# A graph layer on one core: ScalarE issues the stores of the projected rows, and four pieces of an order written by hand move

## The chip, the cores and the metric

The kernel runs on one core of a Trainium2 chip: TensorE (PE), VectorE (DVE), ScalarE (ACT), GpSimd (POOL) and SyncE (SP), each with its own queue that it works through in order, and 16 DMA engines. The metric is the device time of one execution in microseconds. Before the change the median of three runs is 816.37 us (815.54 to 817.31).

## The reference

12,500 nodes with 128 features, 400,000 edges sorted by their destination. Each edge has a length; the weights of an edge come from a two-layer network over 50 radial functions of the length, times a cutoff that is zero beyond a length of 10.

```python
rbf = jnp.exp(-(distances[:, None] - centers) ** 2 / (2.0 * width * width))
cut = 0.5 * (jnp.cos(jnp.pi * distances / CUTOFF) + 1.0) * (distances <= CUTOFF)
W = (jax.nn.silu(rbf @ fw1 + fb1) @ fw2 + fb2) * cut[:, None]
messages = (h[src] @ pw + pb) * W
agg = jax.ops.segment_sum(messages, dst, num_segments=num_atoms)
h1 = h + (jax.nn.silu(agg @ mw1 + mb1) @ mw2 + mb2)
out = layernorm(x + h1)
```

## The kernel before

Only edges with a length up to 10 count. The kernel packs them: seven chunks of rows of edges (`pack(c)`) are compacted on VectorE in log steps (L410 to L439), scattered by POOL to a DRAM tile `packed` (L462), loaded again as `pair` (L479) and turned into four things by place: the indices of the sources `srci` (L533), the destinations within a window `dl` (L556), the window's base `base_i` (L560), and the cutoffs `cut` (L568 to L582). The lengths go back to DRAM as `near_d` (L490), from where they are broadcast to `d` (L656). Chunk 0 uses POOL for the last two transfers, the others SP. `pack` is a generator: each `yield` hands back an estimated time, and a planner advances it piece by piece between other work. `awake[c]` is the planner's time before which chunk c isn't advanced, `clock[0]` its time on VectorE, `pool[0]` that on POOL. The planner decides the order in which each engine gets its instructions; at run time the engines follow that order and wait on semaphores.

The packed edges are worked in quads of 512 (141 of them) and octs of two quads. Quads 0 to 6 belong to chunk 0, 7 to 25 to chunk 1, 26 to 47 to chunk 2 (the third).

The first stage multiplies all node rows by `pw` (`project`, 25 tiles of four times 128 nodes): the x tile is loaded by SP, transposed on TensorE (L595), copied by ScalarE (L597), multiplied (L274, L277), copied to `hp` by ScalarE (L608) and stored to the DRAM tensor `proj` by SP (`node_dma`, L137). `load_x` runs four tiles ahead, `turn` two tiles. The first eight quads are gathered from x itself, so that they need not wait for `proj`; their rows are transposed and multiplied in `multiply`, for four of them between the tiles. In the same loop the planner advances chunks 0 and 1 and the start of chunk 2, and the last four tiles also carry `ahead`: the radial functions of octs 0 and 1 (`basis`: two ScalarE operations over `d`, the second with Exp), their first layer (`first`, L693, on TensorE) and `silu` (L699, ScalarE).

The main loop goes over the quads. For quad q it issues gathers of later quads (L643, four on POOL for each quad, from `proj`, up to eight ahead until quad 24 and four from there; a gather may start when the buffer's last message is done), the second layer of quad q+2 (`second`, L707 and L710), the message (L717), one-hot matrices of the destinations (`place`, L726), the sums by TensorE (`sum_up`, L742) and their addition into `aggT` (L765). At `q % 4 == 3` it calls `basis` for octs q//4\*2+4 and q//4\*2+5; `basis` first drives the planner on (`go_on`) until the chunks of these quads have stored their lengths. The last gathered quads are followed by the node layers and the normalisation, of which most have been spread over the second half of the main loop.

Of the kernel before, what the change touches and what calls it, by code (L numbers as in the profile page):

```python
# [57 lines left out]
def kernel(  # L58
# [37 lines left out]
    nc = tc.nc  # L96
# [21 lines left out]
    def load_x(t0, name="x4", bufs=8):  # L118
        t = work.tile([P, 4, H], F32, name=name, bufs=bufs)
        node_dma(t0, t, x, False)  # L120
        x_sb[t0] = t

    def rows(t0, n=4):
        return [min(P, N - t * P) for t in range(t0, min(t0 + n, NT))]

    def alike(r):


        full = sum(1 for m in r if m == P)
        return [v for v in ((0, full, P), (full, len(r) - full, r[-1])) if v[1]]  # L130

    def node_dma(t0, sb, dr, store):

        for a, m, k in alike(rows(t0)):
            d = dr[(t0 + a) * P:(t0 + a) * P + m * k].rearrange("(t p) f -> p t f", p=k)
            s = sb[:k, a:a + m]
            nc.sync.dma_start(d, s) if store else nc.sync.dma_start(s, d)  # L137

    raw = {}

# [21 lines left out]
    def clear_packed(k, eng):  # L162
        a, b = CLEAR[k:k + 2]
        for i in range(3):
            v = packed[i, a:b].rearrange("(p w) -> p w", p=P)
            for w0 in range(0, (b - a) // P, 376):
                n = min(376, (b - a) // P - w0)
                eng.dma_start(v[:, w0:w0 + n], zero_i[:, :n])
# [6 lines left out]
    def clear(pieces=1, to=N):  # L175

        while pieces and to_clear and to_clear[0][0] < to:
            a, b = to_clear.pop(0)
            nc.scalar.activation(aggT[:, a:b], iota_n[:, :b - a], AF.Copy, scale=0.0)
            pieces -= 1  # L180
# [80 lines left out]
    def part_of(name, t, k, less=True):  # L261

        p = keep.tile([96, H], BF16, name=f"{name}_p{k}")
        nc.scalar.copy(p, t)
        nc.scalar.copy(bias_b[name][32 * k:32 * k + 1],
                       p[32 * k:32 * k + 1, None, :].to_broadcast([1, 4, H]))
        if k < 2 and less:
            nc.vector.tensor_sub(t, t, p)
        return lambda: nc.vector.tensor_sub(t, t, p)

    def rows_times(to, lT, w, bias_b, r):

        for a, c, m in alike(r):
            nc.tensor.matmul(to[:m, a:a + c, :], ones_b[:, :m], bias_b[:, :c, :], start=True,  # L274
                             stop=False)
            for k in range(a, a + c):
                nc.tensor.matmul(to[:m, k, :], lT[:, k * P:k * P + m], w, start=False,  # L277
                                 stop=(k == a + c - 1))
# [22 lines left out]
    proj = dram.tile([N, H], F32, name="proj")  # L301
# [5 lines left out]
    def bank():  # L307

        while not free:
            go_on(held[0])  # L310
        return free.pop(0)
# [29 lines left out]
    clock = [4.2]  # L341
# [3 lines left out]
    awake = [0.0] * NC_  # L345
# [14 lines left out]
    def pack(c):  # L360
# [12 lines left out]
        first = work.tile([P, 1], F32, name="first")  # L373
# [36 lines left out]
        for b in range(bits):  # L410
# [8 lines left out]
            k = 1 << b  # L419
# [126 lines left out]
        if c < WIDE_C:  # L546
# [30 lines left out]
        yield 0.42  # L577
        nc.vector.scalar_tensor_tensor(inside, f_dl, float(W), inside, op0=OP.is_lt, op1=OP.mult,
                                       accum_out=took[:np_, c:c + 1])
        yield 0.42  # L580
        nc.vector.scalar_tensor_tensor(f_cut, f_cut, -1.0, mark, op0=OP.add, op1=OP.mult)
        yield from to_places(f_cut, cut)  # L582
# [18 lines left out]
    def project(t0):  # L601
        r = rows(t0)
        b = bank()
        h = b.rearrange("p (k f) -> p k f", k=4)
        rows_times(h, xT_of.pop(t0), pw_sb, bias_b["pb"], r)
        hp = work.tile([P, 4, H], F32, name="hp", bufs=3)
        for a, c, m in alike(r):
            nc.scalar.copy(hp[:m, a:a + c], h[:m, a:a + c])  # L608
        free.append(b)
        node_dma(t0, hp, proj, True)  # L610

    def multiply(q):

# [34 lines left out]
    def quads(o):  # L648

        return [q for q in (2 * o, 2 * o + 1) if q < NQ]  # L650

    def radial(o, lengths, eng=None):

        d = work.tile([P, QE], F32, name="d", bufs=3)
        for h, ap in enumerate(lengths):
            (eng or nc.sync).dma_start(d[h * 64:h * 64 + 64], ap.to_broadcast([64, QE]))  # L656
        d_of[o] = d, len(lengths)
# [3 lines left out]
    def radials(to):  # L661

        while next_o[0] < min(to, -(-NQ // 2)):
            o = next_o[0]
            if not all(chunk_of(q) in stored for q in quads(o)):
                break
            radial(o, [near_d[2 * q:2 * q + 2].rearrange("(o p) e -> o (p e)", o=1)
                       for q in quads(o)])
            next_o[0] += 1

    def chunk_of(q):
        return max(c for c in range(NC_) if QB[c] <= q)

    def basis(o):
        if o not in d_of:
            for q in quads(o):
                while chunk_of(q) not in stored:
                    go_on(todo[0])
            radials(o + 1)
        d, n = d_of.pop(o)  # L680
        u = n * 64
        rbf = work.tile([P, QE], F32, name="rbf")
        nc.scalar.activation(rbf[:u], d[:u], AF.Square, bias=rbf_bias[:u], scale=rbf_scale[:u])  # L683
        nc.scalar.activation(rbf[:u], rbf[:u], AF.Exp, scale=-1.0 / (2.0 * width * width))  # L684
        rbf_of[o] = rbf, n

    def first(o):

        rbf, n = rbf_of.pop(o)
        ph = ps.tile([P, 2, QE], F32, name="ph", bufs=1)  # L690
        for h in range(n):
            p0 = h * 64
            nc.tensor.matmul(ph[:, h, :], w1_sb[p0:p0 + KR], rbf[p0:p0 + KR], start=True, stop=True)  # L693
        ph_of[o] = ph, n

    def silu(o):
        ph, n = ph_of.pop(o)
        s = work.tile([P, 2, QE], F32, name="s", bufs=3)
        nc.scalar.activation(s[:, :n], ph[:, :n], AF.Silu)  # L699
        for h in range(n):  # L700
            s_of[2 * o + h] = s[:, h]

    def second(q):

        s = s_of.pop(q)
        pu = bank()
        nc.tensor.matmul(pu, ones_b[:, :P], bias_b["fb2"].rearrange("k j f -> k (j f)"), start=True,  # L707
                         stop=False)
        for j in range(QT):
            nc.tensor.matmul(pu[:, j * H:(j + 1) * H], s[:, j * P:(j + 1) * P], fw2_sb,  # L710
                             start=False, stop=(j == QT - 1))
        pu_of[q] = pu
# [236 lines left out]
    tiles = list(range(0, NT, 4))  # L949
    def go_on(c):  # L950
        v = next(chunks[c], None)
        if v is None:
            todo.remove(c)
        else:
            clock[0] += v

    def pack_until(us, among=2):

        while clock[0] < us and todo and todo[0] < among:
            have = [c for c in todo[:2] if c < among]  # L960
            c = next((c for c in have if awake[c] <= clock[0]), None)
            if c is None:
                clock[0] = min([us] + [awake[c] for c in have])
            else:
                go_on(c)
# [18 lines left out]
    tensor = 8.0  # L984

    def ahead(k):

        if k < 2:
            basis(k)
        if k > 1:  # L990
            first(k - 2)
            silu(k - 2)

    for k, t0 in enumerate(tiles):
        if k + AHEAD_X < len(tiles):
            load_x(tiles[k + AHEAD_X])
        if loads and k >= 4 and k % 2 == 0:
            nc.sync.dma_start(*loads.pop(0))
        if k == 12:
            clear_packed(1, nc.sync)  # L1000
        if k in (16, 19, 22):
            if k > 16:
                take_off()
                clock[0] += 0.3
            take_off = part_of("fb2", fb2_f, (k - 16) // 3, False)
        if k == 17:
            load_rows(2)
            awake[2] = tensor + 10.0
        project(t0)
        clear(1, CLEARED)  # L1010
        if k + 2 < len(tiles):
            turn(tiles[k + 2])
        tensor += 2.25
        among = 2 if k < 17 else 3
        pack_until(tensor, among)
        fetches(tensor, FROM_X)
        while times[0] < min(fetched[0], 4) and there_at[times[0]] <= tensor:
            multiply(times[0])
            times[0] += 1
            tensor += 2.1  # L1020
            pack_until(tensor, among)
            fetches(tensor, FROM_X)
        if k in (17, 20, 23):
            radials((k - 14) // 3)
        if k >= len(tiles) - 4:
            ahead(k - len(tiles) + 4)
    while known[0] < QB[2]:
        go_on(todo[0])
    assert not loads
    fetches(clock[0], FROM_X)  # L1030
    for q in (0, 1):
        second(q)
    basis(2)
    basis(3)
    place(0)
# [144 lines left out]
```

## Time and profile before

| | |
|---|---|
| median of three runs | 816.37 us |
| the profiled execution's own time | 819.14 us |
| its span, from first to last instruction | 817.3 us |
| mean granted TensorE clock | 0.851 |
| POOL busy | 569.8 us (70%) |
| TensorE matmul busy | 604.2 us (74%) |
| VectorE busy | 587.5 us (72%) |
| ScalarE busy | 381.1 us (47%) |

No engine is busy all the time. The busy time by stage (microseconds of each engine in each stretch, from the profile's table by windows) shows how the stages differ:

| stretch | PE | DVE | ACT | POOL | PE clock | DMA share |
|---|---|---|---|---|---|---|
| 0 to 41 | 28.6 | 34.0 | 23.5 | 11.6 | 1.00 | 0.80 |
| 41 to 61 | 15.5 | 13.1 | 7.6 | 15.5 | 0.78 | 0.68 |
| 61 to 86 | 17.9 | 7.8 | 18.1 | 12.3 | 0.77 | 0.83 |
| 91 to 135 | 37.3 | 32.4 | 25.1 | 33.5 | 0.96 | 0.44 |
| 135 to 160 | 18.3 | 24.4 | 13.9 | 18.9 | 1.00 | 0.27 |
| 160 to 215 | 42.5 | 49.5 | 23.9 | 42.8 | 0.84 | 0.39 |
| 215 to 785 | 426.5 | 411.0 | 260.5 | 434.7 | 0.85 | 0.38 |

POOL counts as busy only while an instruction runs; between two gathers there is a gap of 0.30 us, so 0.76 of a stretch is POOL without a pause. The projection ends at about 87 us, the main loop's gathers at 785.

### The profile page before, as it was taken

The page shows a single profiled execution, that of the slowest core. Times are in us where ns is not written, and L with a number is a line of the kernel's source. Part 1 is how long each engine was busy: PE and PEld are TensorE (multiplying, and loading weights), DVE is VectorE, ACT ScalarE, POOL GpSimd, SP SyncE. Part 2 cuts the span into 40 slices and gives each one's busy share as a digit, 9 for nine tenths or more (in the row PEclk, how much of TensorE's full clock was granted, in tenths as well). Part 3 has the DMA queues.
Part 4 walks back from the last instruction along what each step waited for, and adds up shares of the span by engine and source line. Part 5 has one row for each costly group of instructions (what it writes and reads, how often), then busy time and mean ns, then how long its engine had stood idle before and what let it go on. Part 6 is the DMA issues. An engine that isn't in the chain of part 4 may idle for free.

```text
span 817.3 us, 11550 instructions
## 1 busy us (share of the span) xinstructions
PE 604.2 (74%) x3492; PEld 475.7 (58%) x3492; DVE 587.5 (72%) x1785; ACT 381.1 (47%) x536; POOL 569.8 (70%) x585
## 2 busy tenths in 40 slices
PE   6777878768776777866588678887777887688661
PEld 5766657547664555655456556665555665566551
DVE  7962568989978877979796677657566565756764
ACT  6536656434644353253354254636444633454421
POOL 1375477777777777777777777777777777777730
PEclk9978899977987776778779788999889989889875
DMA  6968734342234223332531622723622642371221
GB/s 198 263 201 246 191 85 105 90 117 75 74 107 112 65 65 112 103 78 53 144 87 52 164 65 79 194 68 104 170 79 58 159 122 78 80 188 52 81 83 48
DMA packets 88189, 91.86 MB, mean 112 GB/s; under 512 B 13864, under 2 KB 67832, under 8 KB 88120
## 3 DMA queue, kind: packets, MB, share of 16 engines
q1 hardware_dynamic: 69320, 52.77, 22.6%
q0 software_dynamic: 18544, 38.17, 18.6%
q8 instruction: 29, 0.48, 0.2%
q14 instruction: 40, 0.33, 0.1%
q10 hardware_dynamic: 256, 0.11, 0.1%
HBM read 75.29 MB, written 15.71 MB: 111 GB/s over the span
## 4 chain that ended last, share of the span: by engine, by line
DVE 24%; POOL 20%; DMA 20%; issue 16%; PE 14%; ACT 3%; DVEq 2%; SPq 0%; POOLq 0%; ACTq 0%
POOL quad L643 20%; DMA quad<-proj,srci 18%; DVE hot L726 4%; PE sums L742 4%; PE bank L277 3%; DVE aggT L765 3%; DVE quad L726 2%; PE bank L710 2%; DVE msg L717 2%; DVEq L751 2%; PE ph L693 2%; DVE quad L717 1%; DVE r_d L438 1%; DVE nodes L429 1%; PE bank L595 1%
## 5 line engine op out<-in xcount | busy, mean ns | idle before, releaser
L643 POOL DMA_INDIRECT quad<-proj,srci x532 | 524.9, 987 | 169.6 <-issue 131.7
L710 PEld LDWEIGHTS bank<-fw_sb,s 128*128 128x128 f32 x1128 | 175.2, 222 | 37.1 <-issue 28.8
L710 PE MATMUL bank<-fw_sb,s 128*128 128x128 f32 x1128 | 173.5, 304 | 0.0
L699 ACT ACTIVATE s<-ph 128x1024 f32<-128x1024 f32 (+1 forms) x71 | 72.3, 1018 | 197.9 <-PE ph L693 197.8
L742 PEld LDWEIGHTS sums<-hot,msg 128*128 128x128 f32 x696 | 92.3, 206 | 115.4 <-DVE msg L717 84.8
L742 PE MATMUL sums<-hot,msg 128*128 128x128 f32 x696 | 109.3, 304 | 52.6 <-DVE msg L717 52.5
L742 PE MATMUL sums<-quad,quad 128*128 128x128 f32 x432 | 79.3, 342 | 67.8 <-DVE quad L717 67.6
L742 PEld LDWEIGHTS sums<-quad,quad 128*128 128x128 f32 x432 | 70.2, 247 | 74.3 <-DVE quad L717 74.3
L717 DVE TENSOR_TENSOR msg<-bank,quad 128x512 f32<-128x512 f32 x87 | 59.6, 685 | 71.9 <-DMA quad<-proj,srci 62.7
L726 DVE TENSOR_SCALAR hot<-iota_n,dl,cut 128x128 f32<-128x128 f32 x348 | 98.6, 358 | 12.7 <-PE sums L742 8.9
L693 PE MATMUL ph<-rbf,w_sb 51*128 51x512 f32 x282 | 89.5, 711 | 1.5 <-ACT s L699 1.4
L717 DVE TENSOR_TENSOR quad<-bank,quad 128x512 f32<-128x512 f32 x54 | 37.1, 688 | 56.1 <-DMA quad<-proj,srci 54.3
L765 DVE TENSOR_TENSOR aggT<-aggT,sums 128x128 f32 x212 | 60.4, 285 | 22.3 <-PE sums L742 10.9
L707 PE MATMUL bank<-fb_b,ones_b 96*128 96x512 bf16 x141 | 61.5, 436 | 19.3 <-DVE msg L717 8.7
L683 ACT ACTIVATE rbf<-d,rbf_bias,rbf_scale 128x512 f32<-128x512 f32 (+1 forms) x71 | 57.0, 803 | 37.9 <-DMA d<-near_d 37.7
L726 DVE TENSOR_SCALAR quad<-iota_n,dl,cut 128x128 f32<-128x128 f32 x216 | 61.8, 360 | 3.0 <-issue 0.7
L779 ACT ACTIVATE zt<-bank 128x512 f32<-128x512 f32 (+1 forms) x25 | 14.6, 583 | 81.5 <-PE bank L777 81.5
L844 ACT ACTIVATE x<-x,by,rs 128x128 f32<-128x128 f32 x91 | 37.1, 481 | 30.6 <-DVE by L814 30.6
L277 PEld LDWEIGHTS bank<-pw_sb,xT 128*128 128x128 f32 x260 | 40.0, 222 | 11.3 <-issue 5.1
L684 ACT ACT_TABLE_LOAD x36 | 46.2, 1283 | 0.6
L699 ACT ACT_TABLE_LOAD x36 | 46.2, 1283 | 0.6
L684 ACT ACTIVATE rbf<-rbf 128x512 f32<-128x512 f32 (+1 forms) x71 | 44.7, 630 | 1.5
(169 smaller groups left out, 744.2 us busy)
## 6 DMA issues: line engine op xcount, KB each, us to landing
d<-near_d SPq DMA_DIRECT2D x141, 128.0 KB
x<-in_x_dram SPq DMA_DIRECT2D x48, 256.0 KB
quad<-proj,srci POOLq DMA_INDIRECT x532, 2.6
proj<-hp SPq DMA_DIRECT2D x24, 256.0 KB
out_dram<-x SPq DMA_DIRECT2D x24, 256.0 KB
packed<-zero_i SPq DMA_DIRECT2D x6, 188.0 KB
pair<-packed SPq DMA_DIRECT2D x3, 264.0 KB
r_d<-in_edge_weight_dram SPq DMA_DIRECT2D x3, 256.0 KB
```

The lines of the kernel that those rows point to most:

```text
L277: nc.tensor.matmul(to[:m, k, :], lT[:, k * P:k * P + m], w, start=False, stop=(k == a + c - 1))
L643: nc.gpsimd.indirect_dma_start(out=got[:, j, :], out_offset=None, in_=proj if table is None else table, in_offset=bass.IndirectOffsetOnAxi ...
L683: nc.scalar.activation(rbf[:u], d[:u], AF.Square, bias=rbf_bias[:u], scale=rbf_scale[:u])
L684: nc.scalar.activation(rbf[:u], rbf[:u], AF.Exp, scale=-1.0 / (2.0 * width * width))
L693: nc.tensor.matmul(ph[:, h, :], w1_sb[p0:p0 + KR], rbf[p0:p0 + KR], start=True, stop=True)
L699: nc.scalar.activation(s[:, :n], ph[:, :n], AF.Silu)
L707: nc.tensor.matmul(pu, ones_b[:, :P], bias_b["fb2"].rearrange("k j f -> k (j f)"), start=True, stop=False)
L710: nc.tensor.matmul(pu[:, j * H:(j + 1) * H], s[:, j * P:(j + 1) * P], fw2_sb, start=False, stop=(j == QT - 1))
L717: nc.vector.tensor_mul(msg, pu.rearrange("p (j f) -> p j f", j=QT), got_of.pop(q))
L726: nc.vector.tensor_scalar(hot[:, j, :], iota_n[:, :W], dl[:, at[0], at[1]], cut[:, at[0], at[1]], op0=OP.is_equal, op1=OP.mult)
L742: nc.tensor.matmul(pa[:, k * W:(k + 1) * W], msg[:, j, :], hot[:, j, :], start=(j % n == 0), stop=(j % n == n - 1))
L765: nc.vector.tensor_add(to, to, pa[:, k * W:(k + 1) * W])
```

## The change

- `node_dma` takes the issuing engine; `project` passes ScalarE, so that the 26 stores of `proj` are issued from ScalarE's queue, right after the copy to `hp`, and no longer from SP's.
- `ahead` is called at tiles 17, 18 and 19 instead of the last four: at 17 the bases of octs 0 and 1, at 18 and 19 first layer and silu of oct 0 and of oct 1. The loads of their lengths (`radials`) move from tiles 17, 20, 23 to 12, 15 and 23.
- The second layers of quads 0 and 1 move from behind the projection into tile 21. They then stand ahead of the third part of the bias `fb2`, which is written at tile 22, and are computed with its first two bf16 parts.
- When the first chunk's cutoffs are reached, the planner lets that chunk rest for 8 us of its time before it goes on with their transposition.
- The rows of chunk 2 (the third) are loaded at tile 23 instead of 17, and chunk 2 is no longer advanced within the projection.

```diff
-    def node_dma(t0, sb, dr, store):
+    def node_dma(t0, sb, dr, store, eng=nc.sync):
...
-            nc.sync.dma_start(d, s) if store else nc.sync.dma_start(s, d)
+            eng.dma_start(d, s) if store else eng.dma_start(s, d)
...
+        if c == 0:
+            awake[0] = clock[0] + 8.0
...
-        node_dma(t0, hp, proj, True)
+        node_dma(t0, hp, proj, True, nc.scalar)
...
     def ahead(k):
-        if k < 2:
-            basis(k)
-        if k > 1:
-            first(k - 2)
-            silu(k - 2)
+        if k == 0:
+            for o in (0, 1):
+                basis(o)
+        else:
+            first(k - 1)
+            silu(k - 1)
...
-        if k == 17:
+        if k == 23:
             load_rows(2)
-            awake[2] = tensor + 10.0
...
-        among = 2 if k < 17 else 3
-        pack_until(tensor, among)
+        pack_until(tensor)
...
-        if k in (17, 20, 23):
-            radials((k - 14) // 3)
-        if k >= len(tiles) - 4:
-            ahead(k - len(tiles) + 4)
+        if k in (12, 15, 23):
+            radials({12: 1, 15: 2, 23: 3}[k])
+        if 17 <= k < 20:
+            ahead(k - 17)
+        if k == 21:
+            for q in (0, 1):
+                second(q)
...
-    for q in (0, 1):
-        second(q)
```

More of the change, by code (lines that the diff above doesn't have):

```diff
@@ L1020 @@
             tensor += 2.1
-            pack_until(tensor, among)
+            pack_until(tensor)
             fetches(tensor, FROM_X)
-        if k in (17, 20, 23):
-            radials((k - 14) // 3)
-        if k >= len(tiles) - 4:
-            ahead(k - len(tiles) + 4)
+        if k in (12, 15, 23):
[5 more added lines that the diff above has]
+                second(q)
     while known[0] < QB[2]:
```

## The prediction

> **What bounds the kernel now.** I read the table of costly groups first, then the timelines of POOL, ScalarE, TensorE, VectorE and SP around 50 to 200 us (their lines: start, duration, engine, line, operation; in brackets the idle time before and what ended it).
>
> ```profile
> L643 POOL DMA_INDIRECT quad<-proj,srci x532 | 524.9, 987 | 169.6 <-issue 131.7
> ...
> 82.49 0.94 POOL L643 DMA_INDIRECT quad<-in_x_dram,srci  x1 [0.30 <-issue]
> 91.19 1.09 POOL L643 DMA_INDIRECT quad<-proj,srci  x1 [7.76 <-DMA d<-near_d]
> ...
> 159.66 0.99 POOL L462 DMA_INDIRECT packed<-line,at_i  x1 [0.89 <-DVE line L458]
> ```
>
> 532 gathers of about 1.3 us each (0.99 and a 0.30 gap) fill POOL from 91.19 to 785. After its start I find one gap above 0.4 us, the 0.89 before the third chunk's scatter. So two things set the time: when the first gather from `proj` starts, and whether a new gap opens. Afterwards 32 us remain, in which little is gathered.
>
> The first gather needs every store of `proj`, quad 7's gathers, and the message of quad 0, whose buffer it takes. The stage before it:
>
> ```profile
> 67.06 0.39 PE L527 MATMUL bank<-ident,f_cut 14*128 14x14 f32 x2 [3.35 <-DVE f_cut L581]
> ...
> 69.17 2.08 PE L277 MATMUL bank<-pw_sb,xT 128*128 128x128 f32 x8 [0.25 <-ACT xT L597]
> ...
> 86.26 0.80 SPq L137 DMA_DIRECT2D proj<-hp  x2
> ```
>
> TensorE stands still 3.35 us for the first chunk's cutoffs; then 8 matmuls take 2.08 instead of 1.05. The last stores are issued by 87.06; the gather starts 4.1 us later, which I take as their landing (an upper bound, since quad 0's message ends at 90.92).
>
> The third chunk's way to POOL, on VectorE, SP and ScalarE:
>
> ```profile
> 159.09 0.29 DVE L458 TENSOR_TENSOR line<-r_d,there 128x136 int32<-128x136 int32 x1
> ...
> 163.39 0.32 SPq L479 DMA_DIRECT2D pair<-packed  x1
> ...
> 170.64 0.67 DVE L488 TENSOR_TENSOR pair<-pair 44x512 int32<-44x512 int32 x1
> ...
> 177.37 0.81 ACT L683 ACTIVATE rbf<-d,rbf_bias,rbf_scale 128x512 f32<-128x512 f32 x1 [10.30 <-DMA d<-near_d]
> ...
> 179.36 0.24 DVE L529 CAST srci<-bank 128x88 int32<-128x88 f32 x1
> ...
> 186.30 0.69 DVE L717 TENSOR_TENSOR msg<-bank,quad 128x512 f32<-128x512 f32 x1
> ...
> 188.02 1.63 POOL L643 DMA_INDIRECT quad<-proj,srci  x1 [0.30 <-issue]
> ```
>
> 188.02 is quad 26, the first that needs the third chunk's indices, ready at 179.6. The margin is 8.4 us.
>
> **Stores on ScalarE.** 26 issues of about 0.45 us (the two DMA issues at ScalarE's start took 0.42 and 0.45; SP's stores mostly 0.37): 11.7 us. Until 61 us they cost nothing: one tile takes 1.55 us on TensorE, and ScalarE's two copies 1.07, with the issue 1.52. Were that cover gone, they would cost up to 0.45 a tile. SP's loads no longer queue behind stores; TensorE's waits for x after 20 us add to 1 us, and the gathers of quads 0 to 2, which pace 46 to 57 us, hide them.
>
> **The end of the projection, rebuilt from 61.05**, where tile 17's copy starts; the order is that of the built kernel. ScalarE: copy, store, next transpose's copy to 62.7. Two bases, 2 x (0.81 + 0.63), to 65.6 (no table load: nothing has replaced the first table yet). Tile 18's copy, store and transpose's copy to 67.2. The cutoffs still stand ahead of quad 3's copy (table load 1.28, then 0.41 + 0.45), so quad 3's transposed copy ends at 69.95 (before: 69.11). TensorE idles from 64.2, hence 8 matmuls at the slow 2.08: 72.05. First layer of oct 0 at 1.13 or, as at 86.13, 2.08: about 73.6. Project 19 to 75; its copy waits for the Silu load, `silu(0)` and a bias part, and starts at 76.0. Then copy, store, transpose's copy (1.6) and `silu(1)` (1.0) give copies at 78.5 (tile 20) and 80.1 (tile 21), and the transposed copy of tile 23 at 81.65. On TensorE the second layers of quads 0 and 1 (1.11 each, starts 89.98 to 91.09) now stand before projects 22 to 24, from 80.6 to 82.85; the third part of bias fb2 must wait for them on ScalarE, and tile 22's copy behind it. The last three tiles are serial through one bank, about 1.75 each: copies at 84.0, 85.8, 87.75; last store issued at 89.1. With 4.1 to land: 93.2. The other branch: the second chunk's lengths and indices on VectorE now follow the first's cutoffs, indices at 86.4, four gathers of quad 7 to 91.4: not last. Quad 0's message: VectorE passes the second chunk's base first (after project 24) and ends at 90.3: not last. **Start: +2.0.**
>
> Low end: ScalarE's work alone after 61.05 adds to 22 us, stores issued at 84.2, start at 88.3: -2.9. High end: the last two stores also wait, by their semaphores, for the loads of the third chunk's `dst` and `src`, which SP issues behind the second chunk's lengths at about 84. An earlier such load was issued at 59.92 and let VectorE start at 70.71; 10.8 us later than 84 is 94.8, with 4.1 and the issue 99: +8. The next set, issued at 75.73 to 77.17, was passed by 81.8, so I take the short one, which costs nothing here.
>
> A rule speaks here. The Trainium skill, "DMA: Bandwidth & Descriptors", section "Issuing engines are not separate DMA queues", says that DMAs of all issuers interleave on the same 16 engines and a second issuer saves only issue time. The row is the DMA share of 0.83 between 61 and 86 us. By the rule the stores land no sooner; if a queue of their own brought them down in the gathers' median 2.6 us, the start would come at 91.7, +0.5.
>
> **Third chunk's rows later.** Its first five packing steps (2.4 us on VectorE) move into the main loop, and its loads from about 60 to about 84 us. In the built order VectorE writes the scatter's input after 19 messages instead of 16, POOL scatters after 23 quads instead of 21, but VectorE still takes the `pair` after 20 messages: at quad 19 the bases of octs 12 and 13 demand chunk 2's lengths. So three quads of slack become one.
>
> POOL's scatter: 93.2 + 15 x 5.22 (67.9 us for 13 quads, 91.19 to 159.08) = 171.5. VectorE's input: message 8 at about 131.5 (129.69 before), then 18.1 of packing and 20.7 for 11 messages with hots and sums: 170.3. The 0.89 gap goes: **-0.9** (it comes back if VectorE is 2 us later).
>
> From scatter S to the `pair` landed: 3.73 to SP's issue, 0.32, and 2.15 between the 1.58 of the small store at 171.79 (next issue at 173.37) and the 2.9 of the length load behind it: S + 6.2 = 177.7. VectorE is there at about 173 and waits 5 us; behind it stand hots, messages and sums, and on ScalarE oct 13's basis, for whose lengths it waits. Before, 170.64 to 186.30 took 15.66 with 4.9 of packing between; now 5.5: 16.3 to message 22, then 0.6 + hot 1.02 + packing 1.12: indices at S + 25.3. POOL meanwhile does the scatter 1.30 and three quads at 5.41 (160.96 to 188.02 over 5): S + 17.5. **New gap: +7.8.** Low: 2.59 to the issue (55.98 to 58.57), 0.32, 1.58, then 16 in place of 19.1 without the 2.22 that VectorE waited for TensorE before 182.42 and the like: 3.0. High: the second chunk's `pair` took about 9.5 from issue to landing (58.57 to 68.08) in a crowded stage; with 21 on VectorE 17. The DMA share is 0.39 here, so I stay low. POOL never catches up; it has no slack to give.
>
> **Sum.** The profiled run took 819.14 (span 817.3), 2.8 over the median 816.37. 819.14 + 2.0 - 0.9 + 7.8 = 828.0; against the median 825.3.
>
> **Rivals.**
> - B, faster: the projection ends at ScalarE's bound and quad 26 finds its indices: -2.9 - 0.9 = 812.6. For it: the 3.35 stall is gone from TensorE. Against: TensorE idles 5.7 for ScalarE's bases instead, and two second layers moved ahead of the stores. It decides if indices come within 17.5 of the scatter and the last store is issued before 85.
> - C, no change: the start as forecast, the new gap hidden: +2.0 - 0.9 = 817.5. For it: one quad's slack may do if VectorE is late enough. Against: the gap is counted from the scatter itself.
> - D, worse: the last stores wait for the rows (+8) and the gap comes too: +14.9, 831.3.
>
> **How the numbers follow.** Forecast 0.62 (820 to 831 with its bounds), B 0.10, C 0.10, D 0.18. What a measurement can tell is 0.2%, 1.6 us. C falls inside it: faster 0.10, same 0.10, slower 0.80. The range 817 to 832 holds the forecast, C and half of D.
>
> **What would show it.** First `proj` gather near 93; ScalarE's last store near 89; a VectorE wait of some 5 us before L488 of the third chunk; a POOL gap of some 8 us before quad 26, and none before that scatter. A start before 89, or no gap, makes it wrong.

## The result, and the profile after it

The changed kernel takes 821.83 us in the median of five runs (819.49 to 824.22), the kernel before 816.95 us beside it (five runs, 815.54 to 817.99). The ratio is 1.0058, with a 95% interval from 1.0039 to 1.0076: slower by 4.9 us, where the forecast was 8.9. The profiled execution is the quickest of the five: 819.49 us, span 817.7 us. That of the kernel before, 819.14 us with a span of 817.3, took longer than all five runs beside it, so the two profiles lie closer together than the two kernels.

First the changed kernel's table of costly groups (instructions, busy time, mean ns, idle time before), then POOL's timeline.

```profile
L645 POOL DMA_INDIRECT quad<-proj,srci x532 | 521.4, 980 | 170.9 <-issue 130.4
```

```profile
84.19 0.94 POOL L645 DMA_INDIRECT quad<-in_x_dram,srci  x1 [12.80 <-DVE part L541]
...
90.59 0.94 POOL L645 DMA_INDIRECT quad<-proj,srci  x1 [1.67 <-DMA packed<-zero_i]
...
169.10 0.99 POOL L462 DMA_INDIRECT packed<-line,at_i  x1 [0.30 <-issue]
...
192.94 0.94 POOL L645 DMA_INDIRECT quad<-proj,srci  x1 [7.68 <-DVE part L541]
```

The group is the same 532 gathers, 3.5 us shorter in all. The first gather from `proj` comes 0.60 us earlier than before (91.19), the gap of 0.89 ahead of the third chunk's scatter has shrunk to the usual 0.30, and ahead of quad 26, at 192.94 instead of 188.02, POOL now stands for 7.68 us. No other gap above 0.4 us follows the first gather.

VectorE's timeline shows where that gap comes from:

```profile
103.88 0.67 DVE L384 SCALAR_TENSOR_TENSOR step<-drop,gone 128x500 int32<-128x500 f32 x1
111.47 0.16 DVE L392 TENSOR_TENSOR run<-run,cnt 128x1 f32<-128x1 f32 x1 [6.91 <-PE bank L391]
...
164.42 0.29 DVE L458 TENSOR_TENSOR line<-r_d,there 128x136 int32<-128x136 int32 x1
...
175.46 0.68 DVE L488 TENSOR_TENSOR pair<-pair 44x512 int32<-44x512 int32 x1 [8.27 <-DMA pair<-packed]
...
192.42 0.24 DVE L529 CAST srci<-bank 128x88 int32<-128x88 f32 x1
```

The scatter's input is ready at 164.71, but POOL scatters at 169.10, behind 23 quads. VectorE reaches the `pair` before it has landed and waits 8.27 us; the indices of quad 26 follow at 192.66, when POOL has been idle since 185.26. At 111.47 VectorE waits 6.91 us for a sum over partitions that TensorE makes from the results of the first five packing steps, and which stands there behind the work of other quads. In the kernel before those five steps were done in the projection, and the same instruction, at 100.64 in the main loop, waited 0.57 us.

The end of the projection, on TensorE and on ScalarE:

```profile
57.51 1.05 PE L277 MATMUL bank<-pw_sb,xT 128*128 128x128 f32 x8
...
65.65 2.08 PE L277 MATMUL bank<-pw_sb,xT 128*128 128x128 f32 x8 [6.00 <-ACT xT L599]
```

```profile
65.04 0.56 ACT L599 COPY xT<-bank 128x512 f32<-128x512 f32 x1
...
85.13 1.16 ACTq L137 DMA_DIRECT2D proj<-hp  x2
```

TensorE stands 6.00 us for ScalarE's bases and cutoffs and runs slowly after it, as forecast (5.7 and 2.08). Yet the last stores are issued by 86.29, not 89.1, and the gather starts 4.3 us later. The whole stage ran earlier, as the copies of tile 17 show, first before, then changed:

```profile
61.05 0.58 ACT L608 COPY hp<-bank 128x512 f32<-128x512 f32 x1 [2.79 <-PE bank L277]
```

```profile
57.06 0.59 ACT L610 COPY hp<-bank 128x512 f32<-128x512 f32 x1 [1.85 <-PE bank L277]
```

From the first gather to quad 26 the account closes: -0.60 (start), +7.38 (7.68 less the usual 0.30), -0.59 (0.89 less 0.30), -1.30 (the first 72 gathers are shorter) are +4.89; the two profiles differ by 4.92. Behind quad 26 the next 228 gathers are 2.33 us shorter, the last one starts 2.28 us later than before (786.85 against 784.57), and what follows it takes 30.9 us instead of 32.7. So the two profiled spans differ by 0.4 us only, while the medians differ by 4.9.

### The profile page after: what moved, and what is told of

Its sections match the earlier page's. It is cut to its first block, busy times and chain, and to the rows that moved or that the text cites. A ratio compares the mean times of both kernels' runs of the same rounds, so it can differ in the third digit from the quotient of the medians.

```text
span 817.7 us, 11534 instructions
## 1 busy us (share of the span) xinstructions
PE 597.1 (73%) x3492; PEld 467.1 (57%) x3492; DVE 588.1 (72%) x1785; ACT 381.1 (47%) x535; POOL 566.0 (69%) x585
## 4 chain that ended last, share of the span: by engine, by line
DVE 26%; POOL 21%; DMA 20%; issue 17%; PE 11%; DVEq 2%; ACT 2%; SPq 0%; POOLq 0%; ACTq 0%
POOL quad L645 21%; DMA quad<-proj,srci 15%; DVE hot L728 4%; PE sums L744 3%; PE bank L277 3%; DVE aggT L767 3%; DVE quad L728 2%; DVE msg L719 2%; DVEq L753 2%; DVE r_d L438 2%; PE ph L695 1%; DVE quad L719 1%; DVE nodes L429 1%; PE bank L712 1%; DVE go L423 1%
## 5 line engine op out<-in xcount | busy, mean ns | idle before, releaser
L712 PEld LDWEIGHTS bank<-fw_sb,s 128*128 128x128 f32 x1128 | 173.2, 219 | 43.0 <-issue 35.2
L712 PE MATMUL bank<-fw_sb,s 128*128 128x128 f32 x1128 | 171.1, 301 | 0.0
L744 PE MATMUL sums<-quad,quad 128*128 128x128 f32 x432 | 77.4, 336 | 70.8 <-DVE quad L719 70.7
L744 PEld LDWEIGHTS sums<-quad,quad 128*128 128x128 f32 x432 | 68.1, 240 | 77.5 <-DVE quad L719 77.5
L277 PEld LDWEIGHTS bank<-pw_sb,xT 128*128 128x128 f32 x260 | 38.1, 214 | 22.1 <-ACT xT L599 16.5
L277 PE MATMUL bank<-pw_sb,xT 128*128 128x128 f32 x260 | 40.2, 303 | 13.0 <-ACT xT L599 12.9
L645 POOL DMA_INDIRECT quad<-in_x_dram,srci x32 | 32.9, 1027 | 23.0 <-DVE part L541 12.8
```

The lines of the kernel that those rows point to most:

```text
L645: nc.gpsimd.indirect_dma_start(out=got[:, j, :], out_offset=None, in_=proj if table is None else table, in_offset=bass.IndirectOffsetOnAxi ...
L744: nc.tensor.matmul(pa[:, k * W:(k + 1) * W], msg[:, j, :], hot[:, j, :], start=(j % n == 0), stop=(j % n == n - 1))
```

## The experiments

The table gives medians and ratios to the kernel before in the same session, and from each profile: the first gather from `proj`; the quads POOL has gathered before the third chunk's scatter; VectorE's wait for its `pair`; POOL's waits ahead of quads 9 to 15, ahead of that scatter, and ahead of quads 26 and 28 (gaps of 0.5 us or less left out). The changed kernel, e1 to e4, e5 to e8 and e12 were measured in four sessions; rows of different sessions can only be compared by their ratios. The session of e9 to e11 is told apart below.

| kernel | median us | ratio (95%) | first gather | scatter behind | wait for pair | quads 9-15 | scatter | quad 26 | quad 28 |
|---|---|---|---|---|---|---|---|---|---|
| before | 816.95 | 1 | 91.19 | 21 | 0 | 0 | 0.89 | 0 | 0 |
| changed | 821.83 | 1.0058 (1.0039-1.0076) | 90.59 | 23 | 8.27 | 0 | 0 | 7.68 | 0 |
| e1 order back | 828.61 | 1.0142 (1.0100-1.0185) | 99.81 | 21 | 0 | 7.7 | 4.33 | 0 | 0 |
| e2 rows late alone | 819.10 | 1.0025 (0.9998-1.0053) | 87.40 | 22 | 1.53 | 0 | 1.24 | 0 | 3.46 |
| e3 ScalarE stores alone | 821.32 | 1.0050 (1.0025-1.0075) | 95.36 | 21 | 0 | 0 | 0 | 0 | 0 |
| e4 SP stores | 828.00 | 1.0142 (1.0116-1.0167) | 93.07 | 23 | 6.69 | 4.0 | 0 | 8.42 | 0 |
| e5 steps early | 820.52 | 1.0057 (1.0033-1.0082) | 91.56 | 21 | 0 | 5.7 | 0 | 0 | 1.40 |
| e6 before, steps early | 815.30 | 0.9990 (0.9970-1.0009) | 89.70 | 20 | 0 | 1.89 | 0 | 0 | 0 |
| e7 ScalarE stores, rows late | 824.66 | 1.0121 (1.0076-1.0166) | 93.50 | 22 | 2.07 | 0 | 2.54 | 0.99 | 4.83 |
| e8 no rest | 824.61 | 1.0113 (1.0077-1.0149) | 92.59 | 22 | 0.99 | 6.5 | 2.54 | 0 | 3.01 |
| e12 steps spread | 814.86 | 0.9959 (0.9934-0.9984) | 92.78 | 21 | 3.34 | 0 | 0 | 0 | 0 |

**e1: the third chunk's order back.**

```diff
-        if k == 23:
+        if k == 17:
             load_rows(2)
...
+        if k == 22:
+            at = clock[0]
+            for _ in range(5):
+                go_on(2)
+            clock[0] = at
```

> The changed kernel, except that chunk 2's rows are loaded at tile 17 and its first five packing steps are done at tile 22 again, so that POOL's third scatter stands after 21 quads instead of 23 and VectorE's input for it after 17 messages instead of 19. Theory (squeeze): the whole loss is the 7.7 us gap before quad 26. The gap is gone, the 0.9 gap before the scatter may return, the first proj gather stays at 90 to 91, and the time falls from 821.8 to 813 to 816, below the kernel before. Rival (projection): the loss lies in the stores on ScalarE and the moved first layers. Then the time stays at 820 to 823, whether quad 26 waits or not. A POOL that has slack later would also leave it near 820.

The gap ahead of quad 26 is gone, as the theory said. But the kernel is slower still: the first gather comes at 99.81. ScalarE's timeline of this kernel shows the cause, and SP's the transfer behind it:

```profile
63.76 0.57 ACT L610 COPY hp<-bank 128x512 f32<-128x512 f32 x1
71.26 0.37 ACTq L137 DMA_DIRECT2D proj<-hp  x1
71.67 0.58 ACT L599 COPY xT<-bank 128x512 f32<-128x512 f32 x1 [7.34 <-DMA r_d<-in_edge_weight_dram]
```

```profile
59.91 0.49 SPq L147 DMA_DIRECT2D r_d<-in_edge_weight_dram  x1
```

Tile 18 is copied by 64.33, but its store is issued at 71.26. In the built program the store waits not for the copy alone, but also for a DMA semaphore on which it is the ninth transfer; the eighth is the load of chunk 2's lengths, `r_d`, which SP had issued at 59.91 and which the bracket of the next line names too. Behind the store stand the transposed copy, the cutoffs' table load and the rest of ScalarE's queue. TensorE then stands 12.14 us, and the granted clock is 0.57 in 66 to 78 us and 0.50 in 120 to 135, where POOL waits 7.0 us for messages at quads 14 and 15; ahead of the scatter it waits another 4.33 us for VectorE. So putting the rows back at tile 17 was no clean undoing: with the stores on ScalarE the early rows hold ScalarE.

**e2: the rows late, and nothing else.** The kernel before with:

```diff
-        if k == 17:
+        if k == 23:
             load_rows(2)
-            awake[2] = tensor + 10.0
...
-        among = 2 if k < 17 else 3
-        pack_until(tensor, among)
+        pack_until(tensor)
```

> The kernel before, with only chunk 2's rows and first five packing steps later (tile 23, main loop). In the built order POOL's third scatter stands after 22 quads, VectorE's input after 18 messages, the pair still after 20 and the indices after 22 messages. Theory (squeeze): the size of the gap goes by the quads left between the scatter and quad 26. Indices come at about S + 21, POOL is there at S + 23: gap 0 to 3 us, time 816 to 820. Rival (rows on the path): it is the loading itself, whose transfers stand between the last stores of proj; the first gather comes 3 us or more later than 91.2 and the time is 820 or more without a gap before quad 26. Rival (projection): nothing in this part matters, 816 to 818 and no gap at all.

POOL's timeline of this kernel:

```profile
87.40 0.95 POOL L643 DMA_INDIRECT quad<-proj,srci  x1 [8.40 <-DMA d<-near_d]
...
197.84 1.23 POOL L643 DMA_INDIRECT quad<-proj,srci  x1 [3.46 <-DVE msg L717]
```

With one quad more between scatter and quad 26 VectorE waits 1.53 us for the `pair`, not 8.27, and quad 26 finds its indices. The rival of the loading is not borne out: the start is 3.8 us earlier, not later, in this profile, and from tile 17's copy (55.96) to the gather it is 31.4 us, 1.3 more than in the kernel before. But nothing of that reaches the end: quad 28 waits for the message of quad 24, whose buffer it takes, since from here only four quads are ahead. In the kernel before that message ends at 198.7 and quad 28 starts at 199.20: in this stretch an earlier POOL soon runs into VectorE.

**e3: the stores alone.** The kernel before with:

```diff
-        node_dma(t0, hp, proj, True)
+        node_dma(t0, hp, proj, True, nc.scalar)
```

> The kernel before, with only the stores of proj issued from ScalarE. Theory (stores freed the stage): the start of the changed kernel came at 90.6 and not at the forecast 93.2 because the projection ran 3.5 us earlier at tile 17 (hp copy near 57 instead of 61), and that is due to the stores leaving SP. Then tile 17's hp copy starts before 59 and the first proj gather at 87 to 90, time 812 to 816. Rival (clock): the 3.5 us are the granted clock, 1.00 in 50 to 58 us against 0.65; then tile 17's copy falls where the clock of this run puts it, 57 or 61, whatever queue stores, and the time is 816 to 818. Rival (cost): 26 issues of 0.37 to 0.45 us on ScalarE lengthen the end of the projection, first gather after 92, 818 to 820.

The rival of cost is right, by another road than the issues' 0.37 us. Tile 17's copy comes early, at 56.13, but not because of the stores: in e2, where SP stores, it comes at 55.96. ScalarE's timeline, from tile 19's copy on:

```profile
67.90 0.59 ACT L608 COPY hp<-bank 128x512 f32<-128x512 f32 x1 [0.26 <-PE bank L277]
74.92 0.37 ACTq L137 DMA_DIRECT2D proj<-hp  x1
75.33 0.59 ACT L597 COPY xT<-bank 128x512 f32<-128x512 f32 x1 [6.84 <-DMA x<-in_x_dram]
```

Again a store stands 6.4 us behind its copy. Its semaphore's last user is a load of x, which SP issues only after 70.26, because its queue stood behind the loads of `d` from 62.34 on. A wait of SP has become a wait of ScalarE.

**e4: the changed kernel with SP's stores.**

```diff
-        node_dma(t0, hp, proj, True, nc.scalar)
+        node_dma(t0, hp, proj, True)
```

> The changed kernel, except that SP issues the stores of proj again. Theory (squeeze): stores on either queue do not matter for the loss; the gap before quad 26 stays at 6 to 9 us, the time within 2 us of 821.8. If the stores on ScalarE are a gain hidden in the change, the first gather moves from 90.6 to 92 or later and the time to 823 to 826. Rival (ScalarE's issues cost): the first gather comes at 87 to 89 and the time falls to 817 to 820.

```profile
199.73 0.94 POOL L645 DMA_INDIRECT quad<-proj,srci  x1 [8.42 <-DVE part L541]
```

The gap does not depend on the storing queue (8.42 in POOL's timeline). The time does: 828.00. With all else of the change in place the stores on ScalarE are a gain, ratio 1.0058 against 1.0142. On SP the lengths of octs 2 and 3 stand behind the stores (last `d` at 88.27 to 90.9), ScalarE waits 4.99 us for them at 91.45, and POOL 2.26 at quad 9 and 1.74 at quad 13.

**e5: the changed kernel with the third chunk's packing forward.**

```diff
+        if q == 2:
+            for _ in range(8):
+                go_on(2)
```

> The changed kernel, rows of chunk 2 still loaded at tile 23, but after quad 2 of the main loop the planner is made to do chunk 2's first eight packing steps at once. The projection's program stays as it is. In the built order VectorE writes the scatter's input after 16 messages (changed kernel: 19), takes the pair after 19 (20), and POOL scatters after 21 quads (23). Theory (squeeze): start at 90 to 91 as before, no gap before quad 26; VectorE's message of quad 24, at 193 in the kernel before, then holds quad 28 to about 198 against 203.5, so 4 to 6 us are gained of 821.8: 815.5 to 818. Rival (the load itself, or VectorE's extra work in 95 to 135 us): VectorE's messages come late instead and the time stays at 820 to 823.

The gap ahead of quad 26 is gone, and the time is hardly better. POOL's timeline shows what took its place:

```profile
126.33 0.94 POOL L645 DMA_INDIRECT quad<-proj,srci  x1 [1.58 <-DVE msg L719]
...
132.69 1.00 POOL L645 DMA_INDIRECT quad<-proj,srci  x1 [1.54 <-DVE msg L719]
```

Eight steps at once put 8.2 us between the messages of quads 2 and 3 (98.9 and 107.1; changed kernel 2.7), and the quads up to 15 wait for those buffers, 5.7 us in all. The rival, VectorE's messages late, is right for this place of the steps. (Message 24, which my expectation put at 193 in the kernel before, starts there at 198.0.)

**e6: e2 with the same eight steps after quad 2** (the edit of e5, made in e2).

> The kernel before with chunk 2's rows at tile 23 (as in e2_rows_late_alone, whose first gather came at 87.4) and its first eight packing steps forced after quad 2: scatter's input after 15 messages, pair after 18, scatter after 20 quads. Theory (squeeze): the early start is kept and neither quad 26 nor quad 28 waits: 811 to 814. Rival (VectorE's floor): between 150 and 200 us VectorE is the bound whatever the order, message 24 stays at 193, quad 28 near 198, and the time is 815 to 818, as for the kernel before.

Quads 26 and 28 wait no more (message 24 at 189.6 instead of 196.9 in e2), against the rival of a fixed floor. Quad 11 waits 1.89, the start falls at 89.70. 815.30 us are no difference to the kernel before.

**e7: e2 with ScalarE's stores** (the edit of e3, made in e2).

> The kernel before with chunk 2's rows at tile 23 and the stores of proj on ScalarE: the change without the moved first and second layers and without the rest of chunk 0. Theory (shared semaphores): in e1 and e3 a store on ScalarE waited 6 to 7 us for loads of SP that count on the same DMA semaphore, the rows of chunk 2 or what stood behind them. With the rows late ScalarE's stores of tiles 17 to 19 are issued within 1 us of their copies, the first gather comes at 86 to 90, and the time is 815 to 819 with the gap of e2 (0 to 4 us before quads 26 to 28). Rival (ScalarE stores cost by themselves): first gather after 91.5 and 820 or more; then stores wait on ScalarE with the rows late too.

The theory fails here: ratio 1.0121 against e2's 1.0025, first gather at 93.50 against 87.40. ScalarE's timeline, from tile 19's copy on:

```profile
69.45 0.59 ACT L608 COPY hp<-bank 128x512 f32<-128x512 f32 x1 [0.37 <-PE bank L277]
72.94 0.40 ACTq L137 DMA_DIRECT2D proj<-hp  x1
73.37 0.59 ACT L597 COPY xT<-bank 128x512 f32<-128x512 f32 x1 [3.34 <-DMA x<-in_x_dram]
```

The copy ends at 70.04, and its store is issued 2.9 us later, behind a load of x that in the built program counts on the same semaphore. Late rows shorten ScalarE's waits behind SP, they do not end them.

**e8: the changed kernel without the rest of chunk 0.**

```diff
-        if c == 0:
-            awake[0] = clock[0] + 8.0
```

> The changed kernel without the rest of chunk 0 by 8 us. The built order of the third chunk then is that of e2: scatter after 22 quads, input after 18 messages, indices after 22. Theory (squeeze): one quad more of slack, so the gap before quad 26 shrinks from 7.7 to 0 to 4 us and the time falls to 816.5 to 820 if the start stays at 90 to 92. Rival (the rest is what brought the start forward): the cutoffs' transposition stands on TensorE ahead of the projects again with a stall of some 3 us, first gather at 92.5 or later, time 820 to 824.

TensorE's timeline, at the first chunk's cutoffs:

```profile
68.20 0.39 PE L527 MATMUL bank<-ident,f_cut 14*128 14x14 f32 x2 [6.70 <-DVE f_cut L581]
```

The rival is right in the time and half in the reason. The stall is 6.70 us; the start is 92.59. As the theory said, quad 26 does not wait with the scatter behind 22 quads. But POOL waits 6.5 us at quads 14 and 15 and 3.01 at quad 28, with TensorE's granted clock at 0.68 and 0.63 in 105 to 135 us (changed kernel: 0.89 and 1.00), and 2.54 us ahead of the scatter. That the rest brings the start forward is not shown: from tile 17's copy (59.55) to the gather it is 33.0 us here, 33.5 in the changed kernel. This kernel is e7 with the moved layers, and its ratio is the same (1.0113 and 1.0121); no run has the moved layers alone.

**e9, e10, e11: a session at a lower clock.** e9 is the changed kernel unaltered. e10 is it with four packing steps of chunk 2 each after quads 3, 4 and 5; e11 the kernel e2 with three each there:

```diff
+        if q in (3, 4, 5):
+            for _ in range(4):
+                go_on(2)
```

> The changed kernel once more, unaltered, for a second profile: the first was of the fastest of its five executions (819.5 of a median of 821.8). Theory (two costs): the gap before quad 26 stands in every execution, 7 to 9 us; the rest of the spread lies before it, in the start (90 to 93) and in waits of POOL for the messages of quads 3 to 7, whose buffers quads 11 to 15 take: 0 to 5 us, as the changed kernel's relatives e4, e5 and e8 show. Median 820 to 824. Rival: the gap before quad 26 itself varies, and the waits at quads 11 to 15 are absent here too.

> The changed kernel with chunk 2's rows still at tile 23, and four of its packing steps each forced after quads 3, 4 and 5, where VectorE waits for TensorE and ScalarE anyhow, instead of eight at once after quad 2 (e5). Input of the scatter after 14 messages, pair after 18, scatter after 21 quads. Theory (squeeze, and e5 lost by its place): no gap before quad 26, waits of POOL at quads 11 to 15 at most 2 us, 815.5 to 819. Rival (the changed kernel is bound by the messages of quads 4 to 7 whatever stands between them): waits at quads 11 to 15 of 3 us or more, 820 to 822.

> The kernel before with chunk 2's rows at tile 23, stores on SP, and three of chunk 2's packing steps each after quads 3, 4 and 5 (e6 had eight after quad 2 and a wait of 1.9 us at quad 11). Scatter's input after 15 messages, pair after 18, scatter after 21 quads. Theory: the wait at quad 11 goes, none comes at quads 26 and 28, the start is at 87 to 90: 811.5 to 814.5, ratio 0.995 to 0.998. Rival (start by chance): the start falls at 90 to 92 as in the kernel before, 815 to 817, ratio 0.999 to 1.001.

Here the kernel before took 1045.25 us. The view by cores says why, for e9:

```profile
core 0: 1041.3 us, clock 0.759
```

At a granted clock of 0.759 instead of 0.854 the messages bind nearly throughout: in e9 POOL has 35 gaps above 0.5 us between its first gather and 800 us, 12.6 us at quad 13 and 10.2 at quad 26, and at quad 26 e10 and e11 wait 9.7 and 10.1 in spite of their earlier steps. The times expected don't apply. The ratios to the kernel before are 1.0035 (0.9989 to 1.0082) for the changed kernel and 0.9934 (0.9891 to 0.9978) for e11; the runs of e10 give none.

**e12: e10 at the usual clock.**

> The kernel of e10_steps_spread once more: in that call the granted clock was 0.76 for every kernel, the kernel before included, and the times near 1040 us, so the question stayed open for a clock of 0.85. If the kernel before runs at 814 to 818 here: theory (squeeze) gives no gap before quad 26, a first gather at 90 to 93 (the projection is that of the changed kernel, so this is also a second look at its start), waits of POOL at quads 11 to 15 of at most 2 us, 815.5 to 819, ratio 0.999 to 1.003. Rival (the messages of quads 4 to 7 bind the changed kernel whatever stands between them): waits there of 3 us or more, 820 to 822, ratio 1.005 to 1.008. At a clock of 0.76: 0.985 to 0.995, as in e10.

The squeeze theory's signs came, and the time is lower than it said (815.5 to 819, ratio 0.999 to 1.003). POOL's timeline and VectorE's:

```profile
92.78 0.95 POOL L645 DMA_INDIRECT quad<-proj,srci  x1 [1.55 <-DMA packed<-zero_i]
...
161.93 1.18 POOL L462 DMA_INDIRECT packed<-line,at_i  x1 [0.30 <-DVE span L401]
...
200.46 0.95 POOL L645 DMA_INDIRECT quad<-proj,srci  x1 [0.30 <-DVE aggT L767]
```

```profile
168.46 0.69 DVE L488 TENSOR_TENSOR pair<-pair 44x512 int32<-44x512 int32 x1 [3.34 <-DMA pair<-packed]
```

VectorE still waits 3.34 us for the `pair`, but the scatter is five quads ahead of quad 26 and that wait is hidden: after its first gather POOL has no gap above 0.5 us at all. Quad 28 starts 3.0 us earlier than in the changed kernel, although the start is 2.2 later. Median 814.86, ratio 0.9959 (0.9934 to 0.9984): faster than the kernel before, and by the ratios than the changed one.

## Why the forecast was right, and where it was too high

**The new gap: right in kind and size.** "New gap: +7.8" was 7.68 before quad 26 and 8.42 in e4. Its parts stood too: `pair` taken at S + 6.4 (forecast landing S + 6.2), indices at S + 23.6 (25.3), POOL there at S + 16.2 (17.5). VectorE was earlier than worked out: its input came at 164.7 instead of 170.3, so that POOL's place in the order alone set the scatter, and it stood before the `pair` from 167.2 instead of 173, which made its wait 8.27 us instead of 5 without moving the landing. The runs show the dose: with three quads between scatter and quad 26 7.7 and 8.4 us, with four 0, 0.99 and 0 (and 3.0 to 4.8 before quad 28), with five or six none (in e5 1.4 before quad 28). Packing the third chunk earlier, with all else of the change in place (e12), moved the ratio from 1.0058 to 0.9959, by 0.0099 or 8.1 us (both intervals together: 2.5 us either way). That agrees with the gap of 7.4 us beyond the usual 0.30, though the two kernels did not run in one session. Where other waits take its place nothing is won: in e5 the gap is gone too, 7.1 us of waits stand elsewhere, and the ratio is 1.0057.

**The start: the term mis-sized.** "Start: +2.0" was -0.60. The step that failed is its anchor: I rebuilt the stage from 61.05, the profile's time for tile 17's copy, and thereby took that moment as unmoved. In the changed kernel the copy starts at 57.06; in e5 and e12, whose projection is the same program, at 59.89 and 59.25, with the first gather at 91.56 and 92.78. The granted clock goes with it. TensorE between 50 and 58 us, first before, then changed (the clock is the third number from the end):

```profile
50.00:58.00 8.00, 7.27 (x36) 6.52 (x36) 2.21 (x11) 3.48 (x7) 6.17 (x7) 0.65 0.37 110
```

```profile
50.00:58.00 8.00, 6.01 (x51) 5.27 (x50) 3.97 (x19) 4.07 (x8) 5.96 (x7) 1.00 0.31 90
```

Of the eleven profiles outside the session of e9 to e11, four have a clock of 1.00 both in 41 to 50 and in 50 to 58 us, and there the copy starts at 55.96 to 57.50 (changed, e2, e3, e7; in e2 SP stores, in the others ScalarE); in the seven others it starts at 59.13 to 61.05. Why the clock is lower in some executions is not shown. The kernel before has the latest copy of all eleven, so part of the -0.60 is chance. From copy to gather it is 33.5 (changed), 31.7 (e5) and 33.5 us (e12), where the rebuilt stage had 32.15; with the order of before it is 30.1 (before), 31.4 (e2) and 30.6 (e6). As a length the stage was worked out within 1.4 us, and on average it is 2.2 longer, close to the +2.0. Mean start over the three profiles, against the one of before: +0.45.

**The gap before the scatter.** "-0.9" was -0.6: a gather's usual 0.30 stays. Small, but every gap is to be counted less 0.30, the new one too.

**What followed quad 26.** "POOL never catches up; it has no slack to give": from quad 28 to the last gather the distance to the kernel before changes by +0.1 (e1, e7), -0.3 (e5), +1.0 (e3), +2.0 (e4), -2.0 (changed), -2.5 (e12), and by 1.6 or 1.7 either way in e2, e6 and e8. The delays of 4 to 18 us that e1, e3, e7 and e8 bring to quad 28 stand to the end; what varies by 2 us is the gathers' own time. The last 30 us were taken as unmoved and are 1.9 us shorter in the changed kernel (3.4 and 3.1 in e5 and e12). With the terms as measured, 0.45 - 0.6 + 7.4 is 7.3. The median's 4.9 lies 2.4 below it, where the shorter gathers and the shorter end were worth 1.3 + 2.3 + 1.9 in the profiled execution, the quickest of five. How much of this every execution has stays open: the second profile of the changed kernel fell in the session at a lower clock.

**The stores.** "Until 61 us they cost nothing" came out in the sum, but not for the reason given. An issue took 0.37 us, and the cover of 1.55 us a tile was not there: with each of the first six tiles ScalarE also clears a piece of `aggT` (L179), which the forecast's two copies and issue leave out. One tile on ScalarE, first before, then changed:

```profile
18.22 0.59 ACT L608 COPY hp<-bank 128x512 f32<-128x512 f32 x1
18.70 0.62 ACT L179 ACTIVATE aggT<-iota_n 128x500 f32<-128x500 f32 x1
19.22 0.58 ACT L597 COPY xT<-bank 128x512 f32<-128x512 f32 x1
```

```profile
17.55 0.59 ACT L610 COPY hp<-bank 128x512 f32<-128x512 f32 x1
18.17 0.37 ACTq L137 DMA_DIRECT2D proj<-hp  x1
18.58 0.62 ACT L179 ACTIVATE aggT<-iota_n 128x500 f32<-128x500 f32 x1 [0.44 <-ACT hp L610]
19.11 0.57 ACT L599 COPY xT<-bank 128x512 f32<-128x512 f32 x1
```

The next copy to `hp` follows at 19.77 before and at 19.58 in the changed kernel: 1.55 and 2.03 us a tile. TensorE then waits for the first chunk's indices until 31.98 (2.78 us; before 2.52 us until 32.77), and tile 10's copy comes at 33.67 against 34.33, so that this loss is gone again. From the last store's issue to the gather it is 4.3 us, 4.1 before: a second issuer brought no earlier landing. This is in line with the Trainium skill ("DMA: Bandwidth & Descriptors", section "Issuing engines are not separate DMA queues"), by which DMAs of all issuers share the same 16 engines.

**The rivals.** D's mechanism, a store of ScalarE waiting by its semaphore for row loads, exists, but I put it at the wrong place: the late rows, issued at 79.83 to 80.70, held none of the last stores, while the early rows of tile 17 did (e1, 6.9 us). The late rows, which I priced as a loss only, are in the changed order also what makes ScalarE's stores bearable (first gather at 90.59, in e1 at 99.81); in the order of before they are not (e7 1.0121, e3 with early rows 1.0050). B fell with the gap. C needed the gap hidden, and three quads do not hide it.

## What to carry to other kernels

Where a generator's steps are moved, count in the built order how much work of the engine that must not wait lies between the last producer on that engine and its first consumer; here three quads, 16 us of POOL, did not cover a way of 24 us, while five quads, 28 us, had covered the 20 us it took before. Undoing one part of a change is only clean if the parts do not meet: late rows alone cost 0.25%, which is not clear of noise, ScalarE's stores alone 0.50%, both without the moved layers 1.2%, and with all parts and twelve packing steps spread over three quads the kernel gains 0.4%. And an anchor out of one profile carries that execution's clock with it; a stage is better priced as a length, with the start's spread put into the range.

## What the runs showed of the hardware

- An issuing engine can be held by another's queue: stores issued from ScalarE stood 2.9 to 6.9 us behind their copies (e7, e3, e1), waiting for loads on SP's queue that count on the same semaphore.
- The kernel before ran at 815.7 to 817.3 us in four sessions and at 1045.25 us in one; profiles from there show granted clocks of 0.85 and 0.76. The record names another chip for the session at 1045.25 (14) than for e1 to e4 (1), e5 to e8 (13) and e12 (5); whether the clock went with the chip is not shown.
- The granted clock of one stretch differs between executions whose program is the same up to there: between 50 and 58 us 1.00 in e2 and 0.79 in e6, between 41 and 50 us 1.00 in the changed kernel, 0.85 in e5 and 0.81 in e12.
